# Latent attention: scores from two single-pass matmuls over 12-bit halves of q and k, in place of one four-pass matmul with masked k

## The chip, the cores and the metric

The kernel runs on one core of a Trainium2 chip. The metric is the device time of one execution in microseconds, over several runs; lower is better. The profile is of one execution, taken by the hardware profiler. Engines are named as the profile names them: PE (matmuls), PEld (the loads of their weights), DVE (vector), ACT (scalar, activations), POOL and SP (which issues most of the DMAs).

## What is computed

The input x is 8 x 1024 x 256 in fp32. A pre-norm latent attention is added to it, then two layers of local attention with an MLP. Only the first part matters here:

```python
c_kv = x @ W_kv_down                                   # x is layer-normed
k_rope = _rotary_apply(c_kv @ W_k_rope, cos, sin)
k = (c_kv @ W_k_up).reshape(Bb, Tt, NH, HD)            # NH = 16 heads of HD = 16
v = (c_kv @ W_v_up).reshape(Bb, Tt, NH, HD)
q = (x @ W_q).reshape(Bb, Tt, NH, HD)
q_rope = _rotary_apply(x @ W_q_rope, cos, sin)
scores = jnp.einsum('bqhd,bkhd->bhqk', q, k)
scores = scores + jnp.einsum('bqr,bkr->bqk', q_rope, k_rope)[:, None]
scores = scores / scale                                # then causal mask
w = jax.nn.softmax(scores, axis=-1)
attn = jnp.einsum('bhqk,bkhd->bqhd', w, v).reshape(Bb, Tt, D_MODEL)
return attn @ W_o
```

The rotary part is the same for all heads, so the kernel takes exp(rotary part) once per block as `er` and multiplies exp(q.k part) with it.

## The kernel before

`mla` does the latent attention of the eight batches, `local` the two layers after it. `local` isn't touched.

A batch of `mla` is worked off in 36 *steps*, one per entry of `units` (L571 to L577). A unit is one or two parts (c, g, kb): c is the half of the queries (512 columns), g a group of four heads, kb a block of 128 keys. The order is c = 1 with groups 0 and 1 (steps 0 to 12), c = 1 with groups 2 and 3 (13 to 25), c = 0 with groups 0 and 1 (26 to 30), c = 0 with groups 2 and 3 (31 to 35). Most units have one part of 512 columns; in each of the four runs the last three have two parts, 256 and 256 or 384 and 128 columns. All units fill 512 columns, so the exponentials and products after the scores always have the same size.

The order of instructions on PE, DVE, ACT and POOL within the loop is written out by hand (`manual_schedule`, L586). Step s issues:

- `scores` of unit s (L421): four matmuls a part, one for each head n of the group, over 32 rows of q and k each, into four banks of PSUM (two tiles of two banks). Then on ACT two exponentials of 128x1024 (L437) into two `pt` tiles, of which there are six.
- `turned` of unit s - 1 (L441): on DVE two products pt x er of 128x1024 (L451).
- `values` of unit s - 2 (L453): matmuls pt x v into `acc` (L462); where a group ends, ACT copies `acc` out (L470).
- the *beside* work of step s, from the table L518 to L555: projections and transposes of this batch, the next and the one before, spread by hand over the steps.
- `turn_back` and `finished` of groups that have ended (L489, L474), on DVE.

The score banks are used in turn: two tiles for one unit, so the scores of unit s + 1 need the exponentials of unit s.

The projections go through `dense` (L324), which sums into a bank of `psum1` (two banks, tag mm) by four matmuls of 32 columns of weights each (`times`, L198). Of them the change touches `query` and `keys`:

- `query(m, n, c)` (L355) computes heads 8m to 8m + 7 for query half n, and ACT copies the sum into `q` (L360). The weights wq are W_q with its columns put in another order at the start (L248 to L256), so that the 32 rows of a pair hold one head of group 2m (rows 0 to 15) and one of group 2m + 1 (rows 16 to 31).
- `keys(m, n)` (L362) does the same for k, and ACT writes it twice (L372), once per group, each time scaled by a column `mask` that is 1 on the 16 rows of that group's head and 0 on the other's. So each score matmul of 32 rows has 16 rows of zeros.

In a batch, query and keys end in these steps (of the batch in which the step runs): query(1,1) in step 1, keys(1,0) in 3, keys(1,1) in 4, query(0,0) in 5, query(1,0) in 10 for the batch itself; query(0,1) in 22, keys(0,0) in 23, keys(0,1) in 26 for the next one. For the first batch the ones of the second kind run before the loop.

SP issues, in one queue: the loads of x (L188), in step 20 two batches ahead, and the stores of the sums to x2d (L509), in steps 0, 7, 8 and 32. `xn` (the normalised x, L307) and `onat` (L477) have three buffers each.

Of the kernel before, what the change touches and what calls it, by code (L numbers as in the profile page):

```python
# [28 lines left out]

F32 = mybir.dt.float32  # L30
AF = mybir.ActivationFunctionType
ALU = mybir.AluOpType
AX = mybir.AxisListType
PSUM = bass.MemoryType.PSUM

P = 128
D = 256
T = 1024
# [6 lines left out]
NH, HD, DR = 16, 16, 32  # L45
# [36 lines left out]
def preln_mla_local_kernel(  # L82
# [27 lines left out]
    nc = tc.nc  # L110
# [4 lines left out]

    ident = const.tile([P, P], F32, name="ident")
    make_identity(nc, ident)
    half = const.tile([P, 16], F32, name="half")
    nc.gpsimd.memset(half, -0.5)

    x2d = [dram.tile([P, NT, D], F32, tag=f"x2d{b}", name=f"x2d{b}") for b in range(B)]

# [32 lines left out]
    def mla(ctx: ExitStack, verdict):  # L155


        wp = ctx.enter_context(tc.tile_pool(name="w_mla", bufs=1))
        p1 = ctx.enter_context(tc.tile_pool(name="p1", bufs=1))
# [3 lines left out]
        late = ctx.enter_context(tc.tile_pool(name="late", bufs=1))  # L163
# [17 lines left out]
        of = (even, odd)  # L181
        on_v, on_a = Evacuate(nc, "v"), Evacuate(nc, "a")
        HALF = [slice(n * 512, (n + 1) * 512) for n in range(2)]
# [30 lines left out]
        wqnat = wp.tile([P, 2, D], F32, name="wqnat")  # L214
        nc.sync.dma_start(wqnat, W_q.rearrange("(c p) d -> p c d", p=P))
        wknat = wp.tile([P, D], F32, name="wknat")
# [5 lines left out]
        for e in range(2):  # L222
            for r in range(4):
                lo = 32 * r + HD * e
# [10 lines left out]
        for dst, src, plain in ((wqr, wqrope, (1, 1, 0, 0)), (wkr, wkrope.unsqueeze(1), (1, 0, 1, 0))):  # L235
            for n, same in enumerate(plain):
                for a in range(2):
                    lo = (a if same else 1 - a) * HR
                    nc.scalar.copy(dst[:, :, n * DR + a * HR : n * DR + a * HR + HR], src[:, :, lo : lo + HR])

        wq = wp.tile([P, 2, 2, 4, 2, HD], F32, name="wq")
        wk = wp.tile([P, 2, 4, 2, HD], F32, name="wk")
        mask = wp.tile([P, 2], F32, name="mask")
        for e in range(2):
            nc.vector.tensor_reduce(
                mask[:, e : e + 1], ident.rearrange("p (r e d) -> p r e d", e=2, d=HD)[:, :, e, :], AX.XY, ALU.add
            )
        for m in range(2):  # L248
            for e in range(2):
                cols = slice(128 * m + 64 * e, 128 * m + 64 * e + 64)  # L250
                nc.scalar.copy(
                    wq[:, :, m, :, e, :], wqnat[:, :, cols].rearrange("p c (r d) -> p c r d", d=HD)
                )
                nc.scalar.copy(wk[:, m, :, e, :], wknat[:, cols].rearrange("p (r d) -> p r d", d=HD))
        wq = wq.rearrange("p c m r e d -> p c m (r e d)")
        wk = wk.rearrange("p m r e d -> p m (r e d)")  # L256

        vs = []  # L260
        for i in range(2):
            t = of[i].tile([P, NT, NH * VW + 32 - VW], F32, name=f"v{i}")
# [9 lines left out]
        class Batch:  # L272


            def __init__(self, b):
                self.b = b
                self.sums = {}

            def load(self):
                self.x = load_x(self.b) if self.b else first  # L280
# [21 lines left out]
            def normalise(self, n, part):  # L302
                mv, rstd = self.found[n]
                if part == 0:
                    if n == 0:
                        self.xn = []
                    self.xn.append(p1.tile([P, 4, D], F32, tag="xn", name=f"xn{self.b}_{n}", bufs=3))  # L307
                xn = self.xn[n]
                for i in (2 * part, 2 * part + 1):
                    nc.vector.tensor_scalar(  # L310
                        xn[:, i, :], self.x[:, 4 * n + i, :], mv[:, i, 0:1], rstd[:, i : i + 1],
                        ALU.subtract, ALU.mult,
                    )
# [34 lines left out]
            def rope_k(self, n, part=None):  # L348
# [3 lines left out]
                if ps is not None:  # L352
                    nc.vector.tensor_tensor(self.rk[:, HALF[n]], ps, tab[:, 1, HALF[n]], ALU.mult)

            def query(self, m, n, c, part=None):  # L355
                if m == 0 and n == 1 and c == 0 and not part:
                    self.q = of[self.b % 2].tile([P, 2, T], F32, tag="q", name=f"q{self.b}")
                ps = self.dense(f"psq{m}_", [wq[:, 0, m, :], wq[:, 1, m, :]], self.xnc, n, c, part)
                if ps is not None:
                    on_a(self.q[:, m, HALF[n]], ps)  # L360

            def keys(self, m, n, part=None):  # L362

                if n == 0 and not part:
                    if m == 0:
                        self.k = []
                    for e in range(2):
                        g = 2 * m + e
                        self.k.append(of[self.b % 2].tile([P, T], F32, tag=f"k{g}", name=f"k{self.b}_{g}"))
                ps = self.dense(f"psk{m}_", [wk[:, m, :]], [self.ckvT], n, 0, part)  # L370
                for e in range(2) if ps is not None else ():
                    nc.scalar.activation(  # L372
                        self.k[2 * m + e][:, HALF[n]], ps, AF.Identity, scale=mask[:, e : e + 1]
                    )

            def value(self, g, part=None):
                self.v = vs[self.b % 2]
# [24 lines left out]
            def rotary(self, c, kb):  # L402
# [3 lines left out]
                n = 12 * self.b + 8 * (1 - c) + kb  # L406
                nc.scalar.activation(er, ps[:, :w], AF.Exp, scale=SCALE, accum_out=most[:, n : n + 1])  # L407

                nc.scalar.activation(ps[:, :w], ps[:, :w], AF.Exp, scale=-SCALE, accum_out=least[:, n : n + 1])
                if q0 == kb * P:  # L410
# [10 lines left out]
            def scores(self, key, parts):  # L421

                two = [two_banks(f"sc{self.b}_{key}_{i}") for i in range(2)]
                lo = 0
                for c, g, kb in parts:
                    q0, w, _ = self.block(c, kb)
                    for n in range(4):
                        rows = slice(32 * n, 32 * n + 32)
                        nc.tensor.matmul(  # L429
                            two[n // 2][:, n % 2, lo : lo + w], self.k[g][rows, kb * P : (kb + 1) * P],  # L430
                            self.q[rows, g // 2, q0 : q0 + w], start=True, stop=True,
                        )
                    lo += w
                pts = []
                for i, sc in enumerate(two):
                    pt = late.tile([P, 2, 512], F32, tag="pt", name=f"pt{self.b}_{key}_{i}", bufs=6)
                    nc.scalar.activation(pt, sc, AF.Exp, scale=SCALE)  # L437
                    pts.append(pt)
                return pts
# [34 lines left out]
            def finished(self, c, g, oT):  # L474


                nat = late.tile([P, 16, 32], F32, tag="onat", name=f"onat{self.b}_{c}_{g}", bufs=3)  # L477
                nc.vector.transpose(nat.rearrange("p b d -> p (b d)"), oT)
                r = self.rs[:, c, g]
                nc.vector.reciprocal(r, nat[:, :, HD])  # L480
                e = g % 2
                if e == 0:
                    self.onat[c, g // 2] = nat
                nc.vector.tensor_tensor(
                    self.onat[c, g // 2][:, :, HD * e : HD * e + HD], nat[:, :, :HD],
                    r.unsqueeze(2).to_broadcast([P, 16, HD]), ALU.mult,
                )
# [98 lines left out]
        with tc.manual_schedule(engines={E.PE, E.DVE, E.Activation, E.Pool}):  # L586
            for b in range(B + 1):
                for step in range(len(units) if b < B else 9):
# [22 lines left out]
                    if turning:  # L611
                        bt, e = turning.pop(0)
                        bt.turn_back(*e)
                    if done:
                        bt, e = done.pop(0)
# [15 lines left out]
    def local(ctx: ExitStack, verdict):  # L631
# [206 lines left out]
        class Pass:  # L838
# [14 lines left out]
            def qk(self, i):  # L853
# [60 lines left out]
            def scores(self, i):  # L914
# [5 lines left out]
                for g in range(2):  # L920
# [826 lines left out]
    with ExitStack() as one:  # L1747
        mla(one, verdict)
# [9 lines left out]
    with tc.tile_pool(name="psum_v", bufs=1, space=PSUM) as psum:  # L1758
        ps = psum.tile([1, 1], F32, name="psbad")
# [80 lines left out]
```

## Time and profile before

| | us |
|---|---|
| median of three runs | 3350.26 |
| lowest and highest run | 3347.45, 3350.44 |
| span of the profiled execution | 3347.4 |
| end of the latent attention's DVE work in it | about 1010 |
| period of a batch in the latent attention | 121.34 |

The profiled execution's own time isn't given apart from its span, which runs from its first to its last instruction; the lowest of the runs is 0.1 us above that span.

In the profile a group of instructions has a line of kernel.py, an engine, an operation, and its tiles as out<-in; then come busy time and the mean ns of one, and the idle time just before the group with what ended it. An fp32 matmul has two records in PE's groups, each with its own load of weights. Records of PE overlap and their ends are modelled, so the time of a group of matmuls is better read from the start of one to the start of the next. Where the same is done for DVE or ACT, the step from start to start of instructions without a gap is a little below the mean time of one, since their ends overlap too.

### The profile page before, as it was taken

What the parts mean: (1) busy time and instruction counts of PE and PEld (TensorE: products, weight loads), DVE (VectorE), ACT (ScalarE), POOL (GpSimd) and SP (SyncE); (2) the same over time, 40 slices, a digit from 0 to 9 for tenths busy, and PEclk for the clock granted to TensorE, in tenths of its full rate; (3) what the DMA queues carried; (4) which work ended last, traced back from release to release, by engine and by line L of the source; (5) the groups of instructions that cost most, each with busy time, mean ns of one, the idle gap of its engine ahead of it and who ended that gap; (6) DMA issues with size and microseconds to landing.
All of it is one profiled execution on the core that took longest, in us unless ns stands there. A gap on an engine that the chain in (4) does not pass through costs nothing.

```text
span 3347.4 us, 79461 instructions
## 1 busy us (share of the span) xinstructions
PE 3270.7 (98%) x33826; PEld 1777.5 (53%) x33826; DVE 2686.0 (80%) x3993; ACT 1713.1 (51%) x2238; POOL 1341.6 (40%) x1031
## 2 busy tenths in 40 slices
PE   8999999999987899999999999999999999999998
PEld 2433333333333556666565666566666566665665
DVE  5888888888897887888878887777878778787773
ACT  6878878877862244434444434444444444344441
POOL 1000000000006655655655555555555555555540
PEclk9999999999998899999999999999999999999999
DMA  1000000000032444445344354444545444454431
GB/s 63 8 20 27 8 20 27 8 20 14 14 105 81 115 114 120 123 115 143 105 121 127 113 136 130 137 127 136 134 134 139 121 126 130 124 148 119 109 107 58
DMA packets 369290, 311.74 MB, mean 93 GB/s; under 512 B 154607, under 2 KB 333214, under 8 KB 368798
## 3 DMA queue, kind: packets, MB, share of 16 engines
q1 hardware_dynamic: 366942, 304.16, 33.1%
q8 instruction: 268, 4.39, 0.6%
q10 hardware_dynamic: 1984, 2.41, 0.2%
q14 instruction: 96, 0.79, 0.1%
HBM read 165.96 MB, written 140.51 MB: 92 GB/s over the span
## 4 chain that ended last, share of the span: by engine, by line
PE 90%; DVE 3%; ACT 2%; DMA 1%; issue 1%; SPq 1%; POOL 1%; ACTq 0%; DVEq 0%
PE ag L1088 17%; PE pair L859 13%; PE sc L429 9%; PE psy L1129 8%; PE acc L462 8%; PE psw L1005 7%; PE o L972 6%; PE pv L886 6%; PE pair L931 4%; PE psq L200 2%; PE psx L200 2%; PE s L980 2%; PE psR L200 2%; DVE pt L451 1%; PE psy L1135 1%
## 5 line engine op out<-in xcount | busy, mean ns | idle before, releaser
L451 DVE TENSOR_TENSOR pt<-pt,er 128x1024 f32<-128x1024 f32 x576 | 674.8, 1217 | 77.8 <-ACT pt L437 77.8
L437 ACT ACTIVATE pt<-sc 128x1024 f32<-128x1024 f32 x576 | 560.7, 1029 | 174.0 <-PE sc L429 161.6
L1088 PE MATMUL ag<-d,l 128*128 128x512 f32 x1408 | 640.4, 597 | 1.2 <-DVE xs L1009 0.8
L873 POOL TENSOR_TENSOR t<-t,t 128x1024 f32<-128x1024 f32 x128 | 302.0, 2360 | 792.0 <-DVE t L869 792.0
L937 ACT ACT_TABLE_LOAD x120 | 154.0, 1283 | 702.0 <-PE pair L931 702.0
L859 PE MATMUL pair<-l_qkv,xT 128*128 128x512 f32 x1024 | 469.2, 601 | 5.5 <-DMA xT<-zx 2.4
L1088 PEld LDWEIGHTS ag<-d,l 128*128 128x128 f32 x1408 | 262.2, 190 | 310.2 <-issue 278.1
L125 POOL TENSOR_TENSOR rn<-ss,half 128x16 f32<-128x16 f32 x128 | 373.4, 2917 | 13.7
L429 PE MATMUL sc<-q,k 32*128 32x512 f32 (+3 forms) x3072 | 369.9, 522 | 5.1 <-ACT pt L437 5.0
L462 PE MATMUL acc<-pt,v 128*32 128x512 f32 (+3 forms) x3072 | 332.9, 496 | 4.8 <-DVE pt L451 4.6
L859 PEld LDWEIGHTS pair<-l_qkv,xT 128*128 128x128 f32 x1024 | 193.7, 192 | 248.8 <-issue 207.6
L864 ACT ACTIVATE sq<-pair 128x1024 f32<-128x1024 f32 x128 | 131.0, 1023 | 333.2 <-issue 269.1
L866 DVE TENSOR_TENSOR t<-pair,l_cos 128x1024 f32<-128x1024 f32 x128 | 156.2, 1220 | 157.4 <-ACT sq L864 156.7
L1129 PE MATMUL psy<-l,hid 128*128 128x256 f32 x1280 | 281.5, 379 | 0.0
L1101 DVE SCALAR_TENSOR_TENSOR hid<-ag,l_b,ge 128x512 f32<-128x512 f32 x160 | 115.9, 724 | 196.3 <-ACT ge L1100 171.3
L1129 PEld LDWEIGHTS psy<-l,hid 128*128 128x128 f32 x1280 | 243.2, 190 | 46.7 <-issue 15.1
L937 ACT ACTIVATE pt<-pair 128x1024 f32<-128x1024 f32 (+1 forms) x256 | 234.9, 968 | 56.7 <-PE pair L931 55.4
L429 PEld LDWEIGHTS sc<-q,k 32*128 32x128 f32 x3072 | 157.3, 184 | 199.9 <-ACT pt L437 154.3
L411 POOL TENSOR_SCALAR_AFFINE_SELECT er<-er 128x128 f32<-128x128 f32 x64 | 51.5, 804 | 524.0 <-ACT er L407 524.0
L879 POOL TENSOR_TENSOR t<-t,rn 128x1024 f32<-128x1024 f32 x128 | 249.2, 1947 | 10.0
L972 PEld LDWEIGHTS o<-pt,v 128*32 128x32 f32 x7680 | 201.6, 110 | 88.0 <-issue 82.0
L886 PE MATMUL pv<-l_qkv,xT 128*128 128x512 f32 x512 | 240.6, 592 | 0.0
(132 smaller groups left out, 4876.8 us busy)
## 6 DMA issues: line engine op xcount, KB each, us to landing
z<-turned SPq DMA_DIRECT2D x512, 128.0 KB, 2.4
qkT<-z SPq DMA_DIRECT2D x128, 512.0 KB, 3.7
y<-xs SPq DMA_DIRECT2D x128, 128.0 KB, 2.6
h<-y SPq DMA_DIRECT2D x32, 512.0 KB, 4.0
zx<-turneds SPq DMA_DIRECT2D x120, 128.0 KB, 2.7
xT<-zx SPq DMA_DIRECT2D x240, 64.0 KB, 2.6
zh<-turnedh SPq DMA_DIRECT2D x120, 128.0 KB, 2.3
d<-zh SPq DMA_DIRECT2D x30, 512.0 KB, 3.2
```

The lines of the kernel that those rows point to most:

```text
L125: nc.gpsimd.tensor_tensor(out_, in_, half[:, :n], ALU.pow)
L429: nc.tensor.matmul(two[n // 2][:, n % 2, lo : lo + w], self.k[g][rows, kb * P : (kb + 1) * P], self.q[rows, g // 2, q0 : q0 + w], start=Tr ...
L437: nc.scalar.activation(pt, sc, AF.Exp, scale=SCALE)
L451: nc.vector.tensor_tensor(t, t, er.to_broadcast([P, 1024 // w, w]), ALU.mult)
L462: nc.tensor.matmul(self.acc[g][32 * n : 32 * n + 32, q0 - c * 512 :], self.v[:, kb, h * VW : h * VW + 32], pts[n // 2][:, n % 2, lo : lo + w],
L859: nc.tensor.matmul(qk[:, n].rearrange("p h d -> p (h d)"), self.left(i)[c], w["qkv"][:, c, n * INNER : (n + 1) * INNER], start=(c == 0), s ...
L873: nc.gpsimd.tensor_tensor(t1, t1, t2, ALU.add)
L886: nc.tensor.matmul(pv, self.left(i)[c], self.w["qkv"][:, c, 2 * INNER :], start=(c == 0), stop=(c == 1))
L937: nc.scalar.activation(pt[:, :, : n * P], flat[:, :, : n * P], AF.Exp, scale=-1.0)
L972: nc.tensor.matmul(o[32 * j : 32 * j + 32, g, a, :], vs[m][:, h * DH + a * 32 : h * DH + a * 32 + 32], pts[m][g][:, place(j), off : off + ...
L1088: nc.tensor.matmul(ps.rearrange("p (s a t) -> p s a t", a=4, t=32), w["1"][:, c, i, :], d[:, c], start=(c == 0), stop=(c == 1),)
L1129: nc.tensor.matmul(ps[:, t, :], hid[:, i, cols], w["2"][:, i, :], start=(t == i == 0), stop=False)
```

## The change

Scores are still taken for each head over 32 rows, but these rows now hold the head's 16 rows of k in two halves: the value rounded to a type of fewer mantissa bits (float32r, written by ACT) and what is left of it (fp32 minus rounded, written by DVE in the same type). q is split in the same way. One matmul multiplies the 32 rows of k's halves with the low half of q, a second one with the high half, and both add up in the same bank. Both read the operands as float32r.

- `halves` is new: one copy on ACT and one subtraction on DVE from the PSUM bank of the projection, into a tile with two buffers.
- `query` and `keys` call it, and then SP issues 16 DMAs from SBUF to SBUF, each of 16 partitions, which put the halves of each head on its 32 rows: 64 KB each for q (both halves of q, written twice), 32 KB each for k. There are 128 such DMAs in a batch.
- q and k lie in one tile per group and half instead of one per batch or group. All but two of them now have one buffer instead of two.
- The second, masked copy of k and the reordered weights go; W_q and W_k_up are used as loaded.
- `xn` and `onat` have two buffers instead of three.

The diff, cut to its core:

```diff
-        wq = wp.tile([P, 2, 2, 4, 2, HD], F32, name="wq")
-        wk = wp.tile([P, 2, 4, 2, HD], F32, name="wk")
-        mask = wp.tile([P, 2], F32, name="mask")
...
-                nc.scalar.copy(
-                    wq[:, :, m, :, e, :], wqnat[:, :, cols].rearrange("p c (r d) -> p c r d", d=HD)
-                )
-                nc.scalar.copy(wk[:, m, :, e, :], wknat[:, cols].rearrange("p (r d) -> p r d", d=HD))
...
-                    self.xn.append(p1.tile([P, 4, D], F32, tag="xn", name=f"xn{self.b}_{n}", bufs=3))
+                    self.xn.append(p1.tile([P, 4, D], F32, tag="xn", name=f"xn{self.b}_{n}", bufs=2))
...
+            def halves(self, ps, name):
+                t = p1.tile([P, 2, 512], F32R, tag="halves", name=f"{name}{self.b}", bufs=2)
+                on_a(t[:, 0], ps)
+                nc.vector.tensor_tensor(t[:, 1], ps, t[:, 0], ALU.subtract)
+                return t.bitcast(F32)
+
             def query(self, m, n, c, part=None):
-                if m == 0 and n == 1 and c == 0 and not part:
-                    self.q = of[self.b % 2].tile([P, 2, T], F32, tag="q", name=f"q{self.b}")
-                ps = self.dense(f"psq{m}_", [wq[:, 0, m, :], wq[:, 1, m, :]], self.xnc, n, c, part)
-                if ps is not None:
-                    on_a(self.q[:, m, HALF[n]], ps)
+                w = [wqnat[:, i, m * P : (m + 1) * P] for i in range(2)]
+                ps = self.dense(f"psq{m}_", w, self.xnc, n, c, part)
+                if ps is None:
+                    return
+                t = self.halves(ps, f"qh{m}{n}_")
+                for g in (2 * m, 2 * m + 1):
+                    q = of[g % 2].tile([P, 2, 512], F32, tag=f"q{g}{n}", name=f"q{self.b}_{g}_{n}")
+                    for s in range(8):
+                        lo = 64 * (g % 2) + HD * (s // 2)
+                        nc.sync.dma_start(q[HD * s : HD * s + HD], t[lo : lo + HD])
+                    self.q[g, n] = q.bitcast(F32R)
 
             def keys(self, m, n, part=None):
...
-                for e in range(2) if ps is not None else ():
-                    nc.scalar.activation(
-                        self.k[2 * m + e][:, HALF[n]], ps, AF.Identity, scale=mask[:, e : e + 1]
-                    )
+                ps = self.dense(f"psk{m}_", [wknat[:, m * P : (m + 1) * P]], [self.ckvT], n, 0, part)
+                if ps is None:
+                    return
+                t = self.halves(ps, f"kh{m}{n}_")
+                for g in (2 * m, 2 * m + 1):
+                    k = of[self.b % 2 if (m, n) == (0, 0) else 0].tile(
+                        [P, 512], F32, tag=f"k{g}{n}", name=f"k{self.b}_{g}_{n}"
+                    )
+                    for s in range(8):
+                        lo = 64 * (g % 2) + HD * (s // 2)
+                        nc.sync.dma_start(k[HD * s : HD * s + HD], t[lo : lo + HD, s % 2])
+                    self.k[g, n] = k.bitcast(F32R)
...
-                    for n in range(4):
-                        rows = slice(32 * n, 32 * n + 32)
-                        nc.tensor.matmul(
-                            two[n // 2][:, n % 2, lo : lo + w], self.k[g][rows, kb * P : (kb + 1) * P],
-                            self.q[rows, g // 2, q0 : q0 + w], start=True, stop=True,
-                        )
+                    k = self.k[g, kb // 4][:, kb % 4 * P : (kb % 4 + 1) * P]
+                    q = self.q[g, c][:, :, q0 - c * 512 :]
+                    for h in (1, 0):
+                        for n in range(4):
+                            rows = slice(32 * n, 32 * n + 32)
+                            nc.tensor.matmul(
+                                two[n // 2][:, n % 2, lo : lo + w], k[rows], q[rows, h],
+                                start=(h == 1), stop=(h == 0),
+                            )
...
-                nat = late.tile([P, 16, 32], F32, tag="onat", name=f"onat{self.b}_{c}_{g}", bufs=3)
+                nat = late.tile([P, 16, 32], F32, tag="onat", name=f"onat{self.b}_{c}_{g}", bufs=2)
```

More of the change, by code (lines that the diff above doesn't have):

```diff
@@ L30 @@
 F32 = mybir.dt.float32
+F32R = mybir.dt.float32r
 AF = mybir.ActivationFunctionType
@@ L239, in mla @@
                     nc.scalar.copy(dst[:, :, n * DR + a * HR : n * DR + a * HR + HR], src[:, :, lo : lo + HR])
-        wq = wp.tile([P, 2, 2, 4, 2, HD], F32, name="wq")
-        wk = wp.tile([P, 2, 4, 2, HD], F32, name="wk")
-        mask = wp.tile([P, 2], F32, name="mask")
-        for e in range(2):
-            nc.vector.tensor_reduce(
-                mask[:, e : e + 1], ident.rearrange("p (r e d) -> p r e d", e=2, d=HD)[:, :, e, :], AX.XY, ALU.add
-            )
-        for m in range(2):
-            for e in range(2):
-                cols = slice(128 * m + 64 * e, 128 * m + 64 * e + 64)
-                nc.scalar.copy(
-                    wq[:, :, m, :, e, :], wqnat[:, :, cols].rearrange("p c (r d) -> p c r d", d=HD)
-                )
-                nc.scalar.copy(wk[:, m, :, e, :], wknat[:, cols].rearrange("p (r d) -> p r d", d=HD))
-        wq = wq.rearrange("p c m r e d -> p c m (r e d)")
-        wk = wk.rearrange("p m r e d -> p m (r e d)")
         vs = []
@@ L276, in __init__ @@
                 self.b = b
-                self.sums = {}
+                self.sums, self.q, self.k = {}, {}, {}
             def load(self):
@@ L353, in rope_k @@
                     nc.vector.tensor_tensor(self.rk[:, HALF[n]], ps, tab[:, 1, HALF[n]], ALU.mult)
-            def query(self, m, n, c, part=None):
-                if m == 0 and n == 1 and c == 0 and not part:
-                    self.q = of[self.b % 2].tile([P, 2, T], F32, tag="q", name=f"q{self.b}")
-                ps = self.dense(f"psq{m}_", [wq[:, 0, m, :], wq[:, 1, m, :]], self.xnc, n, c, part)
-                if ps is not None:
-                    on_a(self.q[:, m, HALF[n]], ps)
-            def keys(self, m, n, part=None):
[L364 to L370, printed above, removed]
-                for e in range(2) if ps is not None else ():
-                    nc.scalar.activation(
-                        self.k[2 * m + e][:, HALF[n]], ps, AF.Identity, scale=mask[:, e : e + 1]
-                    )
+            def halves(self, ps, name):
[3 more added lines that the diff above has]
+                return t.bitcast(F32)
```

## The prediction

> **What bounds the kernel now.** I read the page's first part, then the busy time of each engine in stretches of one batch, then the timeline of PE, ACT and DVE in that batch, then the groups of instructions and the DMA queue. The change touches only the latent attention, the first 1,005 us of the span; the rest of the kernel stays.
>
> ```profile
> PE 3270.7 (98%) x33826; PEld 1777.5 (53%) x33826; DVE 2686.0 (80%) x3993; ACT 1713.1 (51%) x2238; POOL 1341.6 (40%) x1031
> ```
>
> PE at 98% is an average with modelled ends, so I ask what ends last in each stretch. Batches repeat every 121.34 us (the store of x recurs at 272.93, 394.25 and 515.59 us). I cut one period where the exponentials (L437) of steps 32, 11, 17, 23, 27 and 32 begin. Columns: window, length, then busy us (and instructions) of PE, PEld, DVE, ACT, POOL.
>
> ```profile
> 391.63:442.04 50.41, 50.41 (x556) 19.77 (x560) 47.83 (x68) 37.83 (x51) 2.84 (x4) 1.00 0.13 43
> 442.04:463.45 21.41, 20.41 (x212) 8.25 (x215) 17.20 (x20) 18.44 (x35) 3.75 (x4) 1.00 0.01 1
> 463.45:483.60 20.15, 20.15 (x204) 6.35 (x208) 16.39 (x17) 12.78 (x15) 0.00 (x0) 1.00 0.01 2
> 483.60:496.17 12.57, 12.57 (x152) 5.73 (x155) 11.26 (x18) 11.53 (x15) 1.83 (x1) 1.00 0.01 1
> 496.17:512.97 16.80, 16.80 (x196) 7.16 (x192) 15.01 (x18) 16.35 (x37) 1.08 (x3) 1.00 0.01 3
> ```
>
> I call them A (steps 32 to 35 and 0 to 10), B (11 to 16), C (17 to 22), D (23 to 26), E (27 to 31). A is held by DVE: its timeline runs from 393.5 to 440 us with a single gap of 0.29 us, and PE's weights wait for L451 there. C is held by PE: the next lines, of PE's timeline (start, length), show a step as scores, values, projection, with the next scores close behind.
>
> ```profile
> 465.63 1.14 PE L429 MATMUL sc<-q,k 32*128 32x512 f32 x8
> 466.70 1.06 PE L462 MATMUL acc<-pt,v 128*32 128x512 f32 x8
> 467.59 1.47 PE L200 MATMUL psrq<-xnT,wqr 128*32 128x256 f32 x16
> 468.99 1.14 PE L429 MATMUL sc<-q,k 32*128 32x512 f32 x8
> ```
>
> Start to start: scores 1.07, values 0.89, 768 columns of projection 1.40, together 3.36 us, six times 20.15. E is held by ACT (rotary exponentials L407 and L409 between the pairs of L437). B alternates between PE and ACT; D is nearly level on three engines. The groups of the same period, with the mean ns of one:
>
> ```profile
> L451 DVE TENSOR_TENSOR pt<-pt,er 128x1024 f32<-128x1024 f32 x72 | 84.4, 1217 | 7.6 <-ACT pt L437 7.6
> L437 ACT ACTIVATE pt<-sc 128x1024 f32<-128x1024 f32 x72 | 70.0, 1029 | 20.5 <-PE sc L429 20.4
> L372 ACT ACTIVATE k<-psk,mask 128x512 f32<-128x512 f32 x8 | 5.1, 694 | 0.0
> L346 DVE TENSOR_TENSOR rq<-psrq,tab 128x512 f32<-128x512 f32 x2 | 1.4, 692 | 2.4 <-PE psrq L200 2.4
> L78 ACT COPY q<-psq 128x512 f32<-128x512 f32 x4 | 2.4, 594 | 1.7 <-PE psq L200 1.7
> ```
>
> DVE's sum is 107.7 of 121.3 us, so it has only 13.6 us of room per batch, nearly all of it outside A.
>
> **What the Trainium skill says.** "FP8 and Floating Point Precision", section TensorE Precision Notes: true FP32 takes four passes, while reduced FP32 reads four bytes and truncates. The trace agrees for the four: each score matmul is two records, and a group of four over 512 columns takes 1.07 us. No run yet shows the reduced one. "TensorE: Matmul & The Clock Gate", Back-to-back issue gap, prices a warm pass over 512 columns at 518 cycles, 0.216 us at its 2.4 GHz; four make 0.86, near the 0.89 us of the values. "VectorE: DVE Perf Modes", Why PSUM operands drop a tier: fp32 from PSUM runs in the slowest mode; the trace has 692 ns for 512 columns against 1217 for 1024. "DMA: Bandwidth & Descriptors", Rules for kernel authors: under 64 KB a transfer is mostly overhead; here 64 KB (xT<-zx) lands in 2.6 us and 128 KB (z<-turned) in 2.4.
>
> **The change part by part, per batch.**
>
> *Scores.* Two single passes replace four: 2 x 0.216 = 0.43 us a unit of 512, plus the 0.22 us that the old unit has above its four passes (1.07 - 0.86), plus 0.05 for the second set of weights: 0.70, a gain of 0.37. Bounds: 0.46 (as the values, 0.03 above their passes) and 1.07 (the new type runs no faster). In the 12 units of two parts, 16 short matmuls each need weights that take about 0.18 us to load (184 ns in the record), so I take 0.90 there, a gain of 0.17. Nothing moves in the order of the steps; what is gained counts only where PE ends last.
>
> *DVE.* Eight subtractions a batch (PSUM, 128x512). Nearest row L346, 692 ns; back to back such an operation adds 0.61 us (L508 to L451 start, 407.41 to 408.01). Five of them (steps 1, 3, 4, 5, 10) lie in A, three (22, 23, 26) in C and D. It can't be below nothing: they are extra instructions on an in-order engine.
>
> *ACT.* Four pairs of masked copies (1.16 us a pair, 694 ns each overlapped) become single copies (0.47 as q's, 594 ns alone): -2.8 us. Two of the four are in A and two in D, none where ACT ends last. Copies of q stay. The eight copies of weights at 9 to 12 us go.
>
> *DMA.* 128 transfers a batch on SP, in eight sets of 16. The built program has each wait for the eighth before it. The nearest issue is that of 16 partitions:
>
> ```profile
> L225 SPq DMA_DIRECT2D wout<-in_L_attn_W_o_dram x8: 312/422/432, 5.5 to 12.8; - x8
> L817 SPq DMA_DIRECT2D xT<-zx x240: 517/630/2197, 1108.7 to 3103.9; - x120
> ```
>
> The columns are min, median and max ns. At 0.42 us a set is issued in 6.7 and landed in 9.1 us; eight make 54 of 121 us of SP. The scores use a set at least five steps (16 us) later, which hides it. Behind these transfers in SP's queue stand the loads of x (step 20, queue empty) and the stores of x (steps 7 and 8, late by some us, needed by nobody soon). One place isn't covered: two buffers for halves. The copy of query(0,0) in step 5 overwrites the buffer of keys(1,0) from step 3, and on ACT the exponentials of step 6 stand behind it. From the subtraction of step 3 to the one of step 5 DVE has 2.5 (rest of step 3) + 2.3 + 0.6 + 0.65 + 2.3 = 8.3 us of work; the set lands after 9.1, and copy follows. I charge 0.8 us.
>
> *Buffers of xn and onat, three to two.* All reuse of onat is on DVE in program order; xn is turned in steps 11 to 16, long before the next normalise in step 4. Nothing. If that cover went, a wait on PE of a step, 3 us, would show at L310.
>
> *Sum.* A: five subtractions 3.05, DMA 0.8, less 0.4 for the wait on psx at its front which ends earlier with the scores: +3.4. B: spacings of the exponentials are now 3.60, 4.51, 3.36, 3.26, 2.80, 3.88; carrying the shorter scores through gives 3.50, 4.00, 3.00, 3.29, 2.83, 2.93 (the two in the middle are ACT's own rotary work; in the last, PE comes out of scores earlier and psc, psn follow): -1.9. C: 6 x 0.37 = -2.2. D: DVE 11.26 + 1.22 = 12.5 holds it: -0.3 by carrying. E: ACT's 16.35 stays: -0.4. Net -1.4 us. Six middle batches: -8.4. The first has gaps on DVE in A and nothing of the batch before: -4.8. The last has no next batch, DVE is unbroken from 966 us on: -1. Start-up: its first sets land near 43 and 47 us, where the exponentials of step 1 begin now (47.27), and the first copy of xnT no longer follows weight copies: 0. Sum -14.2 on the profiled 3347.4 us. The span holds all but some tenths of an execution (lowest run 3347.45), and the median of the runs is 2.9 us above: 3350.3 - 14.2 = 3336 us. With scores at 0.46, or the loss in A at 2.5, 3322; with scores at 0.85 or an issue of 0.5, 3350.
>
> **Rivals.**
> 1. *The halves hold ACT (slower).* If an issue costs more than 0.42 us, sets queue: step 1's pushes step 3's, and the copy in step 5 waits. Each 0.1 us costs 1.6 us a batch, more once sets queue; above some 0.53 us the gain is gone. At 0.63, L817's, step 3's set lands after 14.7 us in place of 9.1: 5.6 x 8 = 45 us, 3381. For: one short DMA type costs that. Against: L817 has many small pieces, ours are whole rows, as is the 320 ns store of x (L509).
> 2. *The new type is no faster per column.* Then C, B give nothing, A still costs: about 3375. For: no row of this trace shows a single pass. Against: the skill's account of passes.
> 3. *DVE is the only bound.* 107.7 + 8 x 0.61 = 112.6, with 1.5 us of gaps 114: 7.3 a batch, seven batches 51, 3299. For: A shows DVE without gaps. Against: ACT's rotary work in B and E.
> 4. *It comes out even:* the gain in B and C is eaten by exponentials (1.84 + 0.1 + scores 0.8 + wait = 2.8 a step) and waits for the copy: 3350.
>
> **Numbers.** Forecast 0.52 (0.40 faster, 0.10 same, 0.02 slower), rival 1 0.17 (0.14 slower, 0.03 same), rival 2 0.12 slower, rival 3 0.12 faster, rival 4 0.07 same. Beyond 0.2%, about what a measurement can tell from no change, this gives faster 0.52, same 0.20, slower 0.28. The range 3303 to 3372 leaves out most of rival 2, the worse half of rival 1 and the end of rival 3. The forecast's own range is 3322 to 3350.
>
> **What would show it.** Score units start to next start near 0.70; C near 18 us; A near 54 with DVE without gaps; E as before; 64 new DVE operations near 690 ns; SP issue near 0.4. It is wrong if ACT's copy into halves waits for DMA by more than 3 us a batch, if the score unit stays near 1 us, or if A doesn't grow.

## The result: slower by 2.2%, and the profile after

| | before | after |
|---|---|---|
| median of four runs (lowest to highest), us | 3348.90 (3347.45 to 3350.44) | 3423.18 (3421.14 to 3428.00) |
| ratio, 95% interval | | 1.0224 (1.0210 to 1.0239) |
| span of the profiled execution | 3347.4 | 3422.1 |
| period of a batch | 121.34 | 129.57 |
| first exponential of the second batch | 162.35 | 184.54 |

The forecast was 3336. Of the 74.7 us between the spans, 22.2 are lost by the start of the second batch and 6 x 8.2 = 49.2 in the six batches from there to the start of the last. The few that are left come after the last exponential of the latent attention; they weren't followed.

The same five stretches of one batch (cut at the same exponentials, now L438). Columns: window, length, then busy us (and instructions) of PE, PEld, DVE, ACT, POOL, granted clock, DMA share, GB/s.

```profile
430.82:491.08 60.26, 51.45 (x556) 21.21 (x552) 49.32 (x71) 36.27 (x51) 3.13 (x4) 0.94 0.30 59
491.08:510.89 19.81, 18.69 (x212) 8.03 (x214) 19.01 (x23) 18.45 (x36) 8.31 (x4) 1.00 0.61 129
510.89:528.62 17.73, 17.73 (x204) 6.10 (x207) 15.49 (x17) 12.76 (x14) 0.00 (x0) 1.00 0.08 27
528.62:542.71 14.09, 13.53 (x168) 6.09 (x167) 11.20 (x14) 10.43 (x14) 0.00 (x0) 1.00 0.49 82
542.71:560.39 17.68, 15.85 (x172) 7.39 (x176) 17.37 (x25) 16.17 (x37) 2.29 (x3) 0.90 0.24 50
```

B and C are shorter, as forecast. A is 9.9 us longer and D 1.5. In A, DVE's work grew only from 47.83 to 49.32 us: for some 11 us of it DVE, which the prediction had hold A, stands still. The scores did what they should. In C, from the start of the scores to the start of the values it is now 0.66 us (510.12 to 510.78); it was 1.07:

```profile
510.12 0.74 PE L430 MATMUL sc<-q,k 32*128 32x512 f32 x8
510.78 1.06 PE L463 MATMUL acc<-pt,v 128*32 128x512 f32 x8
511.67 1.04 PE L201 MATMUL psc<-xnT,wkvd 128*32 128x512 f32 x8
```

The idle time of DVE is found in the groups of that batch (busy us, mean ns | idle before it, and what ended it). DVE waits for ACT, and ACT for transfers:

```profile
L344 DVE TENSOR_TENSOR qh<-psq,qh 128x512 fp32r<-128x512 f32 x4 | 2.8, 692 | 10.1 <-ACT qh L79 10.1
L79 ACT CAST qh<-psq 128x512 fp32r<-128x512 f32 x4 | 2.4, 594 | 9.1 <-DMA k<-kh 8.3 <-ACT pt L438 0.4 <-PE psq L201 0.4
L79 ACT CAST kh<-psk 128x512 fp32r<-128x512 f32 x4 | 2.3, 586 | 7.2 <-DMA q<-qh 3.4 <-PE psk L201 2.0 <-DMA k<-kh 1.8
```

SP's timeline of the same A (start, length). From step 1's set on, SP issues for 42 us without a pause:

```profile
450.94 10.03 SPq L357 DMA_DIRECT2D q<-qh  x16
461.06 21.11 SPq L371 DMA_DIRECT2D k<-kh  x32
482.27 11.26 SPq L357 DMA_DIRECT2D q<-qh  x16
```

And ACT's copies in steps 3, 4 and 5, with the exponentials of steps 5 and 6 behind the last two:

```profile
456.55 0.59 ACT L79 CAST kh<-psk 128x512 fp32r<-128x512 f32 x1 [1.98 <-PE psk L201]
...
463.01 0.59 ACT L79 CAST kh<-psk 128x512 fp32r<-128x512 f32 x1 [3.42 <-DMA q<-qh]
463.49 1.95 ACT L438 ACTIVATE pt<-sc 128x1024 f32<-128x1024 f32 x2
473.72 0.59 ACT L79 CAST qh<-psq 128x512 fp32r<-128x512 f32 x1 [8.28 <-DMA k<-kh]
474.20 1.95 ACT L438 ACTIVATE pt<-sc 128x1024 f32<-128x1024 f32 x2
```

The subtraction of step 3 on DVE:

```profile
458.10 0.68 DVE L344 TENSOR_TENSOR kh<-psk,kh 128x512 fp32r<-128x512 f32 x1
```

The exponentials of steps 5 and 6 in the kernel before:

```profile
421.52 1.94 ACT L437 ACTIVATE pt<-sc 128x1024 f32<-128x1024 f32 x2 [0.26 <-PE sc L429]
...
425.43 1.94 ACT L437 ACTIVATE pt<-sc 128x1024 f32<-128x1024 f32 x2 [0.47 <-PE sc L429]
```

Read together: the subtraction of step 3 ends at 458.78, but its set starts at 461.06, when step 1's is through. It is issued until 472.06 and landed at about 473.7, where the copy that waits for it starts: 14.9 us after it was ready. Only then may step 5's copy overwrite its buffer. The exponentials of step 6 stand behind that copy on ACT: they come 10.7 us after those of step 5 (463.49 to 474.20); in the kernel before it was 3.9.

The reason is the time that SP needs to issue one transfer (ns: min, median, max):

```profile
L357 SPq DMA_DIRECT2D q<-qh x512: 507/588/1960, 29.5 to 1022.5; - x171
L371 SPq DMA_DIRECT2D k<-kh x512: 507/587/1882, 39.8 to 999.6; - x171
```

With 45 ns between two it is 0.63 us from start to start, and one or so in a set is longer (1.39 us in step 3's), so a set takes 10 to 11 us, not the 6.7 of the forecast.

### The profile page after: what moved, and what is told of

Same layout as the page of the kernel before. It is cut to its first block, busy times and chain, and to the rows that moved or that the text cites. A ratio compares the mean times of both kernels' runs of the same rounds, so it can differ in the third digit from the quotient of the medians.

```text
span 3422.1 us, 81524 instructions
## 1 busy us (share of the span) xinstructions
PE 3250.0 (95%) x33826; PEld 1787.5 (52%) x33826; DVE 2722.5 (80%) x4055; ACT 1691.5 (49%) x2198; POOL 1374.3 (40%) x1031
## 4 chain that ended last, share of the span: by engine, by line
PE 74%; DVE 10%; SPq 5%; ACT 5%; issue 3%; DMA 2%; POOL 1%; DVEq 0%; ACTq 0%
PE ag L1089 16%; PE pair L860 12%; PE psy L1130 8%; PE psw L1006 7%; PE o L973 6%; PE pv L887 6%; DVE pt L452 5%; PE acc L463 4%; PE pair L932 4%; PE sc L430 3%; SPq L357 3%; SPq L371 2%; ACT pt L438 2%; PE s L981 2%; PE psx L201 1%
## 5 line engine op out<-in xcount | busy, mean ns | idle before, releaser
L438 ACT ACTIVATE pt<-sc 128x1024 f32<-128x1024 f32 x576 | 560.3, 1030 | 123.4 <-PE sc L430 118.2
L463 PE MATMUL acc<-pt,v 128*32 128x512 f32 (+3 forms) x3072 | 404.7, 514 | 27.9 <-DVE pt L452 25.1
L430 PE MATMUL sc<-q,k 32*128 32x512 f32 (+3 forms) x3072 | 263.7, 392 | 70.4 <-ACT pt L438 68.2
L409 POOL TENSOR_SCALAR_AFFINE_SELECT er<-er 128x128 f32<-128x128 f32 x64 | 82.7, 1296 | 551.6 <-ACT er L405 503.9
L430 PEld LDWEIGHTS sc<-q,k 32*128 32x128 f32 x3072 | 141.7, 187 | 262.0 <-ACT pt L438 215.1
```

The lines of the kernel that those rows point to most:

```text
L430: nc.tensor.matmul(two[n // 2][:, n % 2, lo : lo + w], k[rows], q[rows, h], start=(h == 1), stop=(h == 0),)
L463: nc.tensor.matmul(self.acc[g][32 * n : 32 * n + 32, q0 - c * 512 :], self.v[:, kb, h * VW : h * VW + 32], pts[n // 2][:, n % 2, lo : lo + w],
```

## Experiments

Three theories stood. Theory 1: the long issue makes the sets long, they queue on SP, and the two buffers of the halves hand the queue on to ACT. Theory 2: the traffic itself costs the time. Theory 3: DVE's new work does. All times are medians, with the ratio to the kernel before on the same chip; the period is that of a batch in us. "The change" below is the kernel after it; "the strided kernel" is e3.

| kernel | us | ratio (95%) | period |
|---|---|---|---|
| the change | 3423.18 | 1.0224 (1.0210 to 1.0239) | 129.6 |
| e2_two_queues | 3341.96 | 0.9981 (0.9973 to 0.9990) | 119.2 |
| e3_strided | 3334.95 | 0.9959 (0.9945 to 0.9973) | 119.2 |
| f2_spaced | 3360.21 | 1.0034 (1.0021 to 1.0048) | 121.4 to 122.5 |
| e4_no_transfers | 3332.21 | 0.9947 (0.9930 to 0.9963) | 119.2 |
| f3_unread | 3333.05 | 0.9953 (0.9938 to 0.9969) | 119.2 |
| e5_scores_only | 3290.09 | 0.9822 (0.9806 to 0.9838) | 113.8 |
| f4_low_unread | 3335.83 | 0.9960 (0.9945 to 0.9976) | 119.7 |
| f1_pool | 3328.35 | 0.9935 (0.9922 to 0.9949) | 117.8 |
| g3_norm_act | 3347.62 | 0.9999 (0.9991 to 1.0008) | 120.6, one 122.9 |
| g5_norm_early | 3336.09 | 0.9966 (0.9954 to 0.9978) | 119.0, one 120.6 |
| g4_norm_pool | 3341.44 | 0.9979 (0.9969 to 0.9988) | 119.4 to 120.2 |
| g6_norm_early_pool | 3333.93 | 0.9957 (0.9943 to 0.9970) | 117.5, the last 120.9 |

**Half of the issues on another engine (e2)**

```diff
-                        nc.sync.dma_start(q[HD * s : HD * s + HD], t[lo : lo + HD])
+                        (nc.gpsimd if s % 2 else nc.sync).dma_start(q[HD * s : HD * s + HD], t[lo : lo + HD])
```

and the same for k.

> The changed kernel, but of each set of 16 transfers the eight odd ones are issued by POOL, whose queue is nearly empty here, and eight by SP. Theory 1 (SP's 0.63 us an issue makes a set 10.5 us long, the sets of steps 1, 3, 4 and 5 queue, and ACT's copy into one of the two halves buffers waits for them): a set is issued in 5.1 us and landed in 7.4, inside the 8.3 us between two copies that share a buffer; the waits of ACT for DMA fall from about 11 us a batch to under 1, and the time to about 3332 us (3322 to 3345). Theory 2 (the traffic itself, 128 transfers a batch, slows the engines' own reads and writes, or the subtractions on DVE cost more than forecast): the same bytes and operations, so it stays above 3400.

Measured: 3341.96, as theory 1 had it. Between 300 and 1000 us ACT's copies wait for transfers for 9.6 us in all; in the change it is 77.3. That is 1.6 us a batch, where I expected under 1, and 14.3 in the change. POOL's issues are a little shorter than SP's:

```profile
L357 SPq DMA_DIRECT2D q<-qh x256: 507/589/1510, 30.4 to 924.5; - x128
L357 POOL DMA_DIRECT2D q<-qh x256: 484/487/714, 30.7 to 922.6; - x128
```

The Trainium skill says in "Perfetto Trace Analysis", DMA Optimizations, that where the issuing engine's track is full of DMA slices, spreading the transfers over the engines that can issue may help. Here it does: same transfers, same bytes, 81 us less than the change. So the traffic isn't what costs the time, and theory 2 is out.

**A quarter of the issues (e3, the strided kernel)**

```diff
-                    for s in range(8):
-                        lo = 64 * (g % 2) + HD * (s // 2)
-                        nc.sync.dma_start(q[HD * s : HD * s + HD], t[lo : lo + HD])
+                    rows = slice(64 * (g % 2), 64 * (g % 2) + 64)
+                    for s in range(2):
+                        nc.sync.dma_start(q[s::2], t[rows])
```

and so for k. A score sums over a head's 32 rows, so their order is free as long as q and k agree.

> The changed kernel, but the two halves of a head lie on even and odd rows of its 32 instead of on the first and last 16, so that one transfer of 64 partitions to every second partition takes four heads: 4 transfers a set in place of 16, the same bytes. Theory 1a (an issue costs SP a fixed 0.6 us): a set is issued in 2.5 us and landed in 5, no copy waits, about 3330 us (3320 to 3345). Theory 1b (the issue goes with the rows it moves, so 4 times as long): a set takes 10 us again and the time stays near 3420. Theory 2 (traffic or the subtractions): above 3400, with short issues and no wait for DMA.

Measured: 3334.95, and no copy of ACT waits for a transfer between 300 and 1000 us: theory 1a. With four times the rows and bytes, an issue takes the same time:

```profile
L357 SPq DMA_DIRECT2D q<-qh x128: 461/596/1942, 30.3 to 914.9; - x128
L371 SPq DMA_DIRECT2D k<-kh x128: 461/587/1200, 33.6 to 895.7; - x128
```

**The same sets, further apart (f2)**

```diff
-            (0, -1, "out_add", 6, 1, 1), (0, 0, "query", 1, 1, 0),
-            (1, 0, "query", 1, 1, 1),
+            (0, -1, "out_add", 6, 1, 1), (1, 0, "keys", 1, 0),
...
-            (33, 1, "rotary", 1, 4),
-            (34, 1, "rotary", 1, 5), (34, 2, "statistics", 1, 0),
+            (33, 1, "rotary", 1, 4), (33, 1, "query", 1, 1, 0),
+            (34, 1, "query", 1, 1, 1), (34, 1, "rotary", 1, 5), (34, 2, "statistics", 1, 0),
```

The entries of keys(1,0) and query(0,0) in steps 3 to 5 go too, and query(0,0) comes in steps 6 and 7.

> The changed kernel with its 128 transfers and two buffers, and only the steps of the projections moved so that sets come three steps or more apart: query(1,1) to steps 33 and 34 of the batch before, keys(1,0) to 1, keys(1,1) stays at 4, query(0,0) to 6 and 7, query(1,0) stays at 10. Theory 1 (sets of 10.5 us queue when they are asked for every 3.4 us, and two buffers pass the queue on to ACT): the waits of ACT for DMA in the middle batches fall from about 10 to under 2 us, the period from 129.6 to 119 to 121, and the time to about 3355 (3340 to 3370), as the first batch still starts with four sets in a row. Rival (the transfers as such cost): the period stays near 129.

Measured: 3360.21, in the range, with 1.3 us a batch of ACT's waits for transfers (expected under 2); the period is up to 1.5 us above the expected 119 to 121. A is down to 52.5, D stays at 13.7 to 14.2: the sets of steps 22, 23 and 26 weren't spaced. With the transfers unchanged, spacing the sets is thus worth 7 to 8 us a batch. The projections themselves moved with them; what that alone does wasn't measured.

**No transfers (e4), and transfers that nobody waits for (f3)**

```diff
-                t = p1.tile([P, 2, 512], F32R, tag="halves", name=f"{name}{self.b}", bufs=2)
+                tag = name[:4]
+                t = p1.tile([P, 2, 512], F32R, tag=tag, name=f"{name}{self.b}", bufs=2 if tag in ("qh01", "kh00", "kh01") else 1)
...
+                    self.q[g, n] = t.bitcast(F32R)
...
+                    self.k[g, n] = t[:, g % 2].bitcast(F32R)
```

In e4 the transfers are left out. In f3 all 128 a batch are still issued, into tiles that nothing reads.

> The changed kernel with the transfers left out: each projection has its own tile for the halves and the scores read that tile as it stands, so that their products are of other rows than a head's (this part of the computation is changed); PE, DVE and ACT have the same operations. It is the sum of the forecast's parts on the three engines without any transfer. Theory 1: 3330 us (3318 to 3345), a batch of about 119 us, 2.2 less than before. Theory 3 (the eight subtractions in the stretch that DVE holds are what costs): stays above 3390.

> The kernel whose scores read the tiles of the halves as they stand (products of other rows than a head's), with the 128 transfers of 16 partitions put back on SP, into tiles that nobody reads; each projection has its own tile for the halves, so that no copy waits for a transfer. Theory 1 (transfers cost only through the copy that waits for its buffer and through the start): within 4 us of the same kernel without transfers, 3332 to 3336. Theory 2 (traffic or SP's issue slows the engines): above 3350.

Measured: 3332.21 and 3333.05. In f3 SP issues as long as in the change (a set in 10.8 us, three more behind it), but no copy waits. In their middle batches e2, e3, e4 and f3 are the same: A takes 51.7 us in all four, and a batch 119.2. Once nothing waits long for the transfers, they cost nothing there; what sets the four apart lies in the start (the second batch begins at 167.48, 163.45, 156.10 and 155.82 us) and in the last batch. Theory 3 is out too: with all of DVE's new work the kernel is 16 us faster than before. Two stretches of the kernel without transfers, A and E:

```profile
381.81:433.53 51.72, 49.19 (x556) 19.57 (x552) 49.02 (x71) 36.42 (x50) 3.10 (x4) 1.00 0.09 33
...
483.23:500.96 17.73, 17.03 (x200) 7.36 (x202) 17.38 (x25) 16.44 (x37) 2.32 (x3) 1.00 0.01 2
```

**The scores alone (e5), and the subtractions alone (f4)**

```diff
-                    on_a(self.q[:, m, HALF[n]], ps)
+                    on_a(self.q[:, m, HALF[n]].bitcast(F32R), ps)
...
+                    for h in (1, 0):
+                        for n in range(4):
...
+                                start=(h == 1), stop=(h == 0),
```

This is on the kernel before. Both passes go over the same rounded operands, and the exponential takes half the scale; the low halves are left out. For f4 each `query` and `keys` also has one subtraction, into a tile `low` that nothing reads.

> The kernel before with the type of the scores alone changed: ACT writes q and masked k rounded to the shorter type, and each score is taken by two single passes over the same operands, halved in the exponential (the low halves are left out, so the scores are of rounded q and k). No subtraction, no transfer, no other layout. My forecast for the scores without their costs: B -1.9, C -2.2, D about -0.6, E -0.4, A -0.4 a batch, 5.5 in all, about 3311 us (3300 to 3325). Rival 2 (the shorter type is no faster per column): 3349. If a second set of weights eats most of the gain: 3335.

> The kernel with the scores alone changed (of rounded q and k, the low halves left out), plus the eight subtractions a batch on DVE from PSUM into a tile that nobody reads. It prices the subtractions by themselves. If DVE holds the period in all stretches once the scores are short: 8 x 0.66 us a batch, seven batches and a half, about 40 us more than without them, 3330. If only the five in stretch A count, as my forecast had it: 5 x 0.61, about 24 us more, 3314.

Measured: 3290.09, 21 us below what I expected of the scores and outside my range, and 3335.83 with the subtractions, 46 us more (expected 40 or 24). So all eight subtractions count, not only the five in A: (119.7 - 113.8) / 8 is 0.74 us each. It is above their 0.61 as ACT's second copy of k also waited for them in that kernel (28.9 us between 300 and 1000 us). Between e4 and e5, which differ in ACT's copies too, it is (119.15 - 113.78) / 8 = 0.67. The scores alone, A and E:

```profile
366.89:415.36 48.47, 47.27 (x556) 20.17 (x552) 46.85 (x68) 37.81 (x53) 3.58 (x4) 1.00 0.10 35
...
464.71:480.67 15.96, 14.55 (x192) 6.53 (x188) 14.94 (x18) 15.96 (x37) 1.58 (x3) 1.00 0.01 2
```

Without the subtractions A is 3.3 us shorter than in e4 and E 1.8.

**The subtractions on POOL (f1)**

```diff
-                nc.vector.tensor_tensor(t[:, 1], ps, t[:, 0], ALU.subtract)
+                raw = p1.tile([P, 512], F32, tag="raw", name=f"raw{name}{self.b}")
+                on_a(raw, ps)
+                nc.gpsimd.tensor_tensor(t[:, 1], raw, t[:, 0], ALU.subtract)
```

This is on the strided kernel.

> The kernel with strided transfers, and the subtraction moved from DVE to POOL: ACT copies each projection twice, once rounded and once in full into a tile of its own, and POOL subtracts from that one. Two small weights and the last verdict's tile lie in other buffers to make the room. DVE's busy time of a batch goes from 112.4 back to about 107.7 us, ACT's from 94.1 to about 98. Theory (DVE is what holds the period at 119.1 us once nothing waits for transfers, each subtraction costs its 0.66 us in full): the period falls to about 113.8, that of the kernel with the scores alone changed, and the time to about 3296 us (3288 to 3308). Rival (it isn't DVE: ACT's extra copies or PE hold the period, or POOL slows DVE's products by using the same memory): 3320 or more, or the mean of L452 well above 1217 ns.

Measured: 3328.35, where the rival had it. The mean of DVE's products pt x er rose from 1218 to 1281 ns. Over the 72 of a batch that is 4.5 us, of the 5.4 that eight subtractions cost at 0.67. DVE beside POOL, first DVE, then POOL:

```profile
413.70 3.43 DVE L454 TENSOR_TENSOR pt<-pt,er 128x1024 f32<-128x1024 f32 x2
417.05 0.72 DVE L292 TENSOR_SCALAR xn<-x,mv,rstd 128x256 f32<-128x256 f32 x2
417.69 2.35 DVE L454 TENSOR_TENSOR pt<-pt,er 128x1024 f32<-128x1024 f32 x2
```

```profile
414.74 1.31 POOL L346 TENSOR_TENSOR kh<-rawkh,kh 128x512 fp32r<-128x512 f32 x1 [1.23 <-ACT rawkh L79]
```

A pair of products takes 2.35 us, and 3.43 if POOL subtracts meanwhile: here DVE loses 1.08 of POOL's 1.31 us, more than the 0.67 that it was spared. The Trainium skill says why in "SBUF — State Buffer", SBUF: two separate sides: a DVE operation with two inputs in SBUF and an operation of GpSimd (here POOL) that reads SBUF take one pair of ports in turn, each for its whole length. The trace agrees: where POOL has to wait instead, its subtraction takes up to 4.76 us, and DVE loses 0.2 to 0.3. In A DVE is busy for 51.1 of 51.9 us. What is gained comes from D and E (28.2 us together in place of 29.9).

**Other work off DVE (g3 to g6)**

```diff
-                    nc.vector.tensor_scalar(
-                        xn[:, i, :], self.x[:, 4 * n + i, :], mv[:, i, 0:1], rstd[:, i : i + 1],
-                        ALU.subtract, ALU.mult,
+                    nc.scalar.activation(
+                        xn[:, i, :], self.x[:, 4 * n + i, :], AF.Identity,
+                        bias=mv[:, i, 0:1], scale=rstd[:, i : i + 1],
                     )
```

The bias is worked out on DVE at the start of `normalise` (g3, g4), or on POOL at the end of `statistics` (g5, g6). g3 and g5 start from the strided kernel, g4 and g6 from f1.

> The kernel with strided transfers and the subtractions on DVE, and instead the eight normalisations a batch (L292, 128x256, 405 ns, 0.33 us each without a gap), which all lie in stretch A, moved from DVE to ACT, with one small DVE operation more in each half. Theory (A is held by DVE alone and ACT has more than 10 us of room there): 8 x 0.33 less about 0.15 is 2.5 us a batch, the period falls from 119.15 to about 116.6, and the time from 3335 to about 3317 us (3310 to 3325). Rival (ACT's added copies come between the exponentials and hold the scores back, or PE is the next bound just below DVE): 3328 or more.

> The kernel with the subtractions on POOL (3328 us), and the normalisations on ACT as well. There DVE's products are slowed from 1219 to 1281 ns while POOL works, which eats most of what the subtractions gave back. Theory (DVE still holds A in that kernel, by these slower products): 2.3 us a batch less, about 3311 us (3303 to 3320). Rival (in that kernel ACT or PE already holds A, since ACT has a second copy of each projection): within 5 us of 3328.

> The kernel with strided transfers and the normalisations on ACT, but the bias that they need comes from POOL right after the statistics, some steps earlier, instead of from DVE in the same step. In the run before, ACT stood 20.5 us in five and a half batches for that DVE operation, which is queued behind DVE's backlog in A, and the period rose from 119.15 to 120.6. Theory (the loss there was that wait of ACT, the same kind as the changed kernel's wait for transfers): the wait goes and the period falls to 116.5 to 117.5, the time to about 3320 us (3312 to 3328). Rival (the normalisations, 598 ns each on ACT, fill ACT between the exponentials by themselves): the period stays at 119 or above, 3335 or more.

> The same with the subtractions on POOL as well. Theory: without the wait (11.8 us in the run before) this comes below the kernel with the subtractions on POOL alone (3328 us), at about 3318 (3308 to 3326). Rival (with two copies of each projection and the normalisations, ACT holds A): 3332 or more.

The measured times are 3347.62, 3341.44, 3336.09 and 3333.93, in the order g3, g4, g5, g6. None went with the theory; g3, g5 and g6 came out where the rival had them, g4 above both. For g6 this holds of the time alone: in the middle its period, 117.5, isn't above f1's 117.8, but its second batch begins at 168.45 us in place of 161.66. In g3 ACT waits in step 4 for a DVE operation of 0.15 us that is queued behind DVE's backlog, and with it wait the exponentials:

```profile
426.78 1.09 ACT L293 ACTIVATE xn<-x,mv,rstd 128x256 f32<-128x256 f32 x2 [3.81 <-DVE mv L290]
```

In g5 that wait is gone, and the time is still that of the strided kernel. DVE has less to do in A (48.06 us in place of about 49), but A stays at 51.6. Taken step by step against the strided kernel, steps 6 and 7 are 1.8 us shorter, and steps 5 and 10, in which ACT does the moved work, 1.7 longer. In each of the two longer steps a pair of moved normalisations stands on ACT right before the exponentials that open the next step (at 426.55 and 442.00):

```profile
425.55 1.09 ACT L294 ACTIVATE xn<-x,mv,rstd 128x256 f32<-128x256 f32 x2
...
441.00 1.10 ACT L294 ACTIVATE xn<-x,mv,rstd 128x256 f32<-128x256 f32 x2
```

So DVE's relief shortened the steps that DVE held, and ACT's new work lengthened others by as much.

## Why the prediction was wrong, point by point

- **The step that failed is the transfers' price**: "At 0.42 us a set is issued in 6.7 and landed in 9.1 us", and with it "I charge 0.8 us". An issue took 0.63 us from start to start, a set 10 to 11, and step 3's set landed 14.9 us after it was ready. In place of that 0.8, A is 8.5 us longer than without transfers, and ACT's copies waited 14.3 us a batch in all, where my own sign of being wrong was 3. The landing, 2.4 us after the issue, was nearly right (2.3 and 2.0). The 6.7 also left out the time between two issues: the last of L225's start 0.47 us apart (11.86, 12.33, 12.80), not 0.42. I took the price from L225 and set aside L817 in the same fence, with a median of 630 ns, because of its "many small pieces". The strided run shows that rows and bytes don't set it; the number of pieces wasn't varied. Both rows are of loads from DRAM and ours go from SBUF to SBUF, so neither was near enough to be taken alone; the dearer one would have been the safer forecast.
- **Rival 1 is what happened**, and its 14.7 us for step 3's set at 0.63 was right. Its total, 3381, was too low because it charged one wait a batch, and nothing at the start. Against the kernel without transfers, A is 8.5 us longer and D 1.9: step 4's copy waits too (3.4 us, for step 1's set), and so does the later copy of keys in D (1.8).
- **Start-up at 0** was wrong, for the most part by the same price. The first two sets are issued until 39.70 and 49.95 us, three sets before the loop and four in it follow each other on SP, and step 1's exponentials begin at 56.61 in place of 47.27. The second batch starts at 184.54 us (before: 162.35), without transfers at 156.10. Even the strided kernel has 163.45.
- **Scores** at 0.70: 0.66. C: -2.4 (forecast -2.2), B: -1.6 (-1.9).
- **The sum without the wait** was -2.2 us a batch; the kernel without transfers has 121.34 - 119.15 = 2.19. That is partly luck. A grew by 1.3 in place of 2.65 (3.05 less 0.4), as DVE takes part of the new work along into B (busy for 17.20 us before, 18.98 without transfers), and E, forecast at -0.4, grew by 0.9. "A is held by DVE" was too strong: the shorter scores alone took 1.9 us from A. And of the three subtractions of steps 22, 23 and 26 I charged two to D and none to E; DVE carries them as backlog into E, where it is then busy for 17.38 of 17.73 us.
- **ACT -2.8**: 96.9 to 94.1 us a batch. **DVE**: 107.7 to 112.4, eight operations of 690 ns. Both as forecast.
- **Rival 2** (no faster per column) is out by the 0.66. **Rival 3** (DVE the only bound, 114 us a batch) is out by the 119.15: DVE is then busy for 112.1 us, and the period is 7 longer. Rival 4 didn't come about.
- What holds A at 51.6 to 51.9 us once the waits are gone: in f1 DVE, slowed by POOL. In the strided kernel DVE has hardly a gap from step 2 to step 7, and holds these:

```profile
408.43:431.86 23.43, 21.44 (x196) 7.05 (x192) 23.19 (x38) 13.76 (x17) 1.01 (x1) 1.00 0.62 137
```

From there to A's end, 8.93 us, PE works without a pause. In g5 it is part DVE, part ACT's moved work, as shown above. For g4 and g6 it stays open.

The strided kernel and the one with POOL leave nothing out, and both are faster than the kernel before and the change, at 0.9959 and 0.9935 of the kernel before; their intervals just overlap.

## What to carry to other kernels

Price many small transfers by the issuing engine's time for each, from start to start, by the dearest of the near rows if none is of the same kind, and lay the sets on that queue in order of time: what counts is when the last one in the queue lands, and which in-order engine waits to reuse its buffer. Fewer, larger transfers cured it here, and a free choice of row order allowed them. Lay out the start of the kernel in the same way: no earlier work covered the first sets here. Before work is moved off a full engine, ask what the receiving engine holds up while it does it, and with whom it shares ports.

## What the runs showed of the hardware that was not expected

- An issue on SP from SBUF to SBUF took 587 to 596 ns in the median, with 16 or 64 partitions and 32 to 256 KB alike; one on POOL 487. Loads from DRAM took 422 (L225) and 630 (L817 of the kernel before). What sets it stays open.
- If an fp32 matmul takes four passes, as the prediction has it, a single pass in the shorter type costs about the same: two single-pass sets of four over 512 columns take 0.66 us and an fp32 set 1.07, which is 0.2 for each of the two passes between them; the values take 0.89, which is 0.22 a pass. The load of weights didn't get shorter (183 ns in the median, 184 before).
- A normalisation of 128x256 took 598 ns on ACT and 405 on DVE.
- The granted clock of A was 0.94 in the change and 1.00 without transfers. It is 0.50 from 474 to 477 us, right after the long wait, in which PE worked for 0.20 of 5 us (469 to 474). A matmul of the values over 512 columns took 1.06 us in its record just after that (477.35) and about 0.6 later (482.03). So PE was slower for a while after such a wait, too.
